# Expert rows beyond 256 in pieces of 128, and the values of two contexts computed in the router's gap

## The chip, the cores and the metric

The kernel runs on one core of one Trainium2 chip. The metric is the device time of one execution in microseconds; the figure before the change is the median of three runs. A profile is one such execution taken apart by the hardware profiler, with its own span. The engines are named as in the profile: PE is TensorE's matmul, PEld its weight load, DVE is VectorE, ACT ScalarE, POOL GpSimd, and SP SyncE, which here only issues DMAs.

## What is computed

Two decoder layers over x (B = 4 sequences of S = 512 rows, D = 256 columns, fp32), each with a layer normalization after every residual addition. The second attention of both layers looks at a context of S2 = 1601 rows per sequence. The feed-forward part of the first layer is a mixture of eight experts, of which each row uses two. Cut to what the change touches:

```python
# layer 0, mixture of experts, 2048 rows
probs = softmax(x @ Wr + br)                      # 8 experts
topw, topi = top_k(probs, 2); topw /= sum(topw)
def expert(x, e):                                 # FF = 1024
    h = gelu(x @ Wi[e] + bi[e]) * sigmoid(x @ Wg[e] + bg[e])
    r = x + (h @ Wo[e] + bo[e])
    return normalized(r) * gamma[e] + beta[e]
x = layernorm(x + sum over the two picks of topw * expert(x, pick))
# layer 1, self attention (16 heads of 16), then cross attention
Q = rope(x @ Wq.T + bq); K = rope(ctx @ Wk.T + bk); V = ctx @ Wv.T + bv
x = layernorm(x + softmax(mask(Q K^T / 4)) V @ Wo.T + bo)
# then a feed-forward part with dequantized weights
```

## The kernel before, in words

The stages follow one another in time: the first attention of layer 0 (0 to about 153 us of the span), its cross attention with the router of each sequence (to 487), a gap in which the last router result is turned into lists of rows (to 523), the experts (to 1023), the self and cross attention of layer 1 (to 2286), and the last feed-forward part (to 2438). Expert, cross-attention and self-attention stages are written under a manual schedule: each engine runs its instructions in the order in which the program issues them.

**Router and lists.** `route(b)` (L457) computes the logits of sequence b on PE, picks two experts per row on DVE, and multiplies the picks with a triangular matrix (L507) to rank each row within its expert. `scatter(b)` (L528) then writes the rows of x to a list `xs` in DRAM, one region of 2048 rows per expert, with eight indirect DMAs that POOL issues (L534). For the last sequence nothing else fills PE meanwhile. `blocks_left` (L539) counts what each expert has beyond its first 256 rows, and makes the tables `wrow` (which expert's weights) and `xrow` (which rows) of the dynamic blocks, and `yrows`, with which layer 1 fetches its results.

**Blocks.** Every expert has one block of 256 rows whose place is known (8 "first" blocks), and 15 dynamic blocks of 256 rows go where the counts say: 23 in all, however the rows fall. A block needs three weight tiles of its expert: eWi and eWg (1028 KB each, biases behind the matrix) and eWo (1408 KB, with bo, gamma and beta behind it). For a first block SP loads them from a fixed place; for a dynamic block POOL issues indirect DMAs (L397). The functions per block are:

- `begin(i)` (L830): the loads of the rows, xb, and of eWi and eWg. The rows are issued first.
- `turned` (L849): four transposes of xb on PE (L854), copied to xbT by DVE.
- `first_half` (L861): issues the load of eWo; then eWi and eWg times xbT, 256 columns wide, Gelu and Sigmoid on ACT (L883), their product on DVE (L886), and the addition of bo to xb on POOL (L889).
- `second_half` (L892): g times eWo into one bank, the residual addition on DVE (L899), the normalization, gamma and beta on POOL (L910, L911), and the store to `ys` by SP (L912).

The loop (L1002 to L1016) interleaves them: loads of block i+1, first half of block i, transposes of block i+1, second half of block i-1. The buffers are two for each weight, three for xb. So a block's weights arrive while the block before is computed, and `attention_first`, a generator of small preparations for layer 1, is advanced once per block.

**Values of the contexts.** Layer 1's cross attention runs in units (b, g): sequence b, a group g of four heads. Side work is cut into items that are spread over the units in lists named `extras` and `quiet`; loads stand in `starts`. `context(b, keys, values)` (L1173) makes the items of context b: `key` projects, rotates and stores a chunk of keys; `value` (L1186) projects 128 rows of the context with the weight xaV and copies them to `vals[b % 2]` (ACT, L1191). Contexts 0 and 1 are done early; in `later` (L1613) the keys of contexts 2 and 3 and their values, 13 tiles each, are spread over the cross units of b = 0, 1 and 2. A tile takes two matmul calls, four PE passes as the profile counts them, of 256 columns.

Of the kernel before, what the change touches and what calls it, by code (L numbers as in the profile page):

```python
# [9 lines left out]
F32 = mybir.dt.float32  # L10
# [29 lines left out]
def decoder(ctx: ExitStack, tc: tile.TileContext, a: dict, out: bass.AP):  # L40
# [345 lines left out]
    NDYN = 2 * B * S // BLK - 1  # L386
    ys = tc.dram_tile(((E + NDYN) * BLK, D), F32, name="ys")

# [28 lines left out]
    for name, n in (("iota", E), ("base", E), ("more", E - 1), ("upto", E * E), ("dyn", NDYN), ("p", 2)):  # L417
        fields[name] = cmoe[:, at_ : at_ + n]
        at_ += n
# [119 lines left out]
    def blocks_left():  # L539
# [5 lines left out]
        more = prt.tile([P, E, E - 1], F32, tag="more", name="more")  # L545
        nc.vector.tensor_tensor(
            more,
            n[:, :, None].to_broadcast([P, E, E - 1]),
            fields["more"][:, None, :].to_broadcast([P, E, E - 1]),
# [4 lines left out]
        upto = prt.tile([P, E, E], F32, tag="upto", name="upto")  # L554
# [8 lines left out]
        past = prt.tile([P, NDYN, E], F32, tag="past", name="past")  # L563
# [12 lines left out]
        nc.vector.tensor_scalar(j, j, 1.0, float(E - 1), ALU.add, ALU.min)  # L576
# [4 lines left out]
        nc.vector.tensor_scalar(xf, j, float(BLK), None, ALU.mult)  # L581
# [5 lines left out]
        xrow = prt.tile([P, 2, NDYN], I32, tag="xrow", name="xrow")  # L587
        for h in range(2):
            nc.vector.tensor_scalar(xrow[:, h, :], xf, fields["p"][:, h : h + 1], None, ALU.add)
# [6 lines left out]
        nc.vector.tensor_tensor(yf, yf, eks, ALU.subtract)  # L596
# [8 lines left out]
        return wrow, xrow  # L605


    with tc.tile_pool(name="p2", bufs=2) as p2, ExitStack() as ordered:
# [135 lines left out]

        def tail():
            if tails and next(tails[0], tails) is tails:
                tails.pop(0)
# [21 lines left out]
        while tails:  # L769
            tail()  # L770
        ordered.close()
        scatter(B - 1, lambda inst: unordered("xs", inst))
        wrow, xrow = blocks_left()
# [8 lines left out]
    VW = HD + 1  # L782
# [38 lines left out]
    with tc.tile_pool(name="p3", bufs=2) as p3, ExitStack() as ordered:  # L821
# [8 lines left out]
        def begin(i):  # L830

            e = i if i < E else wrow[:, i - E : i - E + 1]
            xb = p3.tile([P, 2, D], F32, tag="xb", name="xb", bufs=3)
            if i < E:
                nc.sync.dma_start(
                    xb, xs[i * B * S : i * B * S + BLK, :].rearrange("(h p) d -> p h d", p=P)
                )
            else:
                for h in range(2):
                    nc.gpsimd.indirect_dma_start(  # L840
                        xb[:, h, :],
                        None,
                        xs,
                        bass.IndirectOffsetOnAxis(ap=xrow[:, h, i - E : i - E + 1], axis=0),
                    )
            wi, wg = expert_first[i] if i < 2 else load_expert(e, expert_in, pmw)
            return i, e, wi, wg, xb

        def turned(i, e, wi, wg, xb):  # L849
            ps = bank()  # L850
            pv = ps.rearrange("p (c n) -> p c n", c=2)
            for c in range(2):
                for h in range(2):
                    nc.tensor.transpose(  # L854
                        pv[:, c, h * P : (h + 1) * P], xb[:, h, c * P : (c + 1) * P], ident
                    )
            xbT = p3.tile([P, 2, BLK], F32, tag="xbT", name="xbT")
            nc.vector.tensor_copy(xbT, pv)  # L858
            return i, e, wi, wg, xb, xbT

        def first_half(i, e, wi, wg, xb, xbT):  # L861

            (wo,) = load_expert(e, ("eWo",), p3)
            g = p3.tile([P, NF, BLK], F32, tag="g", name="g")
            for w, func in ((wi, AF.Gelu), (wg, AF.Sigmoid)):
                for f0 in range(0, NF, 4):
                    ps = wide()
                    pv = ps.rearrange("p a (h n) -> p (a h) n", n=BLK)
                    dst = g[:, f0 : f0 + 4, :]
                    if w is wg:  # L870
                        dst = p3.tile([P, 4, BLK], F32, tag="sg", name="sg")
                    for k in range(4):
                        f = f0 + k
# [3 lines left out]
                                (w[:, c * FF + f * P : c * FF + (f + 1) * P], xbT[:, c, :])  # L877
# [3 lines left out]
                    for k in range(4):  # L881
                        bias = w[:, 2 * FF + f0 + k : 2 * FF + f0 + k + 1]
                        nc.scalar.activation(dst[:, k, :], pv[:, k, :], func, bias=bias)  # L883
                    if w is wg:
                        part = g[:, f0 : f0 + 4, :]
                        nc.vector.tensor_tensor(part, part, dst, ALU.mult)  # L886

            bo = wo[:, None, NF * D : NF * D + D].to_broadcast([P, 2, D])
            nc.gpsimd.tensor_tensor(xb, xb, bo, ALU.add)  # L889
            return i, wo, xb, g  # L890

        def second_half(i, wo, xb, g):  # L892
            ps = bank()
            pv = ps.rearrange("p (h d) -> p h d", d=D)
            for h in range(2):
                blk = slice(h * P, (h + 1) * P)
                mm(pv[:, h, :], [(g[:, f, blk], wo[:, f * D : (f + 1) * D]) for f in range(NF)])
            r = p3.tile([P, 2, D], F32, tag="rb", name="rb")
            nc.vector.tensor_tensor(r, pv, xb, ALU.add)  # L899
            mv = moments(r, 2)  # L900
            rs = rstd_of(mv, eps12, 2)
            for h in range(2):
                nc.vector.tensor_scalar(
                    r[:, h, :], r[:, h, :], mv[:, h, 0:1], rs[:, h : h + 1], ALU.subtract, ALU.mult
                )
            gam, bet = (
                wo[:, None, (NF + k) * D : (NF + k + 1) * D].to_broadcast([P, 2, D]) for k in (1, 2)
            )
            eng = nc.vector if i == E + NDYN - 1 else nc.gpsimd
            eng.tensor_tensor(r, r, gam, ALU.mult)  # L910
            eng.tensor_tensor(r, r, bet, ALU.add)  # L911
            nc.sync.dma_start(ys[i * BLK : (i + 1) * BLK, :].rearrange("(h p) d -> p h d", p=P), r)  # L912
# [87 lines left out]
        ready = {}  # L1000
        ordered.enter_context(tc.manual_schedule())
        n = E + NDYN  # L1002
        read = [begin(0), begin(1)]
        more = attention_first()
        begun = first_half(*turned(*read.pop(0)))
        nxt = turned(*read.pop(0))
        for i in range(1, n):
            if i + 1 < n:
                read.append(begin(i + 1))
            half = first_half(*nxt)  # L1010
            if i + 1 < n:
                nxt = turned(*read.pop(0))
            second_half(*begun)
            begun = half
            next(more, None)
        second_half(*begun)  # L1016
# [9 lines left out]
    with ExitStack() as s4:  # L1026
# [146 lines left out]
        def context(b, keys, values, here=None):  # L1173
# [20 lines left out]
            for i in sorted({*keys, *values}):  # L1194
# [5 lines left out]
                eng = nc.gpsimd if here is None else nc.vector  # L1200
# [403 lines left out]
        for f in keys0[0:2] + values1 + add + keys0[4:6] + turn:  # L1604
            f()
# [5 lines left out]
        for i, (n0, n1) in enumerate(((0, 4), (4, 6), (6, 7), (7, 8))):  # L1611
            extras[i] = ([k1_, q1_, rows1] if i == 0 else []) + keys1[n0:n1] + extras[i]
        later = [  # L1613
            context(2, range(4), ()) + context(3, range(2), ()),
            context(3, range(2, 4), ()) + context(2, (), range(4)),
            context(3, (), range(4)),
        ]
# [124 lines left out]
def _constants():  # L1742
# [11 lines left out]
    ndyn = 2 * B * S // (2 * P) - 1  # L1754
# [3 lines left out]
        np.arange(1, E) * 2 * P,  # L1758
# [95 lines left out]
```

## Time and profile before

| | |
|---|---|
| median of three runs | 2437.68 us (2436.15 to 2438.79) |
| the profiled execution, whole | 2439.88 us |
| its span | 2438.0 us |
| its mean granted clock | 0.97 |
| PE busy | 2344.4 us (96%) |
| DMA | 215.84 MB, mean 89 GB/s |

The second part of the page shows the span in 40 slices, about 61 us each, busy tenths per slice:

```profile
PE   7898999959999999989999999999999999999998
PEclk9999999969999999989999997999999999999999
DMA  8300311145667555351211210112110110100100
GB/s 307 150 1 3 124 54 45 49 143 186 247 239 266 198 204 201 124 164 50 66 48 35 95 36 5 39 51 60 51 37 16 45 36 16 30 34 18 31 9 26
```

PE is full almost everywhere; the slice with a 5, the ninth, holds the router's gap, and there the granted clock is lower too. The experts are the slices nine to seventeen, where the DMA engines work most.

A line of a timeline below gives the start, the length, the engine, the line of the kernel and the operation, the output tile and the inputs, the shape, and in brackets how long the engine had been idle before it and who released it. A pass of the expert matmuls is short, so the length of a group of them, from one group's start to the next one's, is the better measure: the ends are modelled, and a printed length overlaps the next group a little.

### The profile page before, as it was taken

To read this page: it belongs to the slowest core of one execution; us is meant where nothing else is said; L and a number is where in the kernel's file an instruction comes from. 1 tells how busy PE (TensorE), PEld (TensorE's weight loads), DVE (VectorE), ACT (ScalarE), POOL (GpSimd) and SP (SyncE) were. 2 spreads that over 40 slices of the span, in tenths; PEclk is the share of its full clock that TensorE was granted. 3 is DMA by queue.
4 is the path that set the end of the run, shared out by engine and by line. 5 is a ranking of instruction groups with operands and counts; after the bars stand their busy time and mean duration, and the time that the engine had idled before them with its cause. 6 is when DMAs were issued, how large, how long until landed. Compare 5 with 4: busy or idle time off the path is not lost.

```text
span 2438.0 us, 34867 instructions
## 1 busy us (share of the span) xinstructions
PE 2344.4 (96%) x13928; PEld 1328.2 (54%) x13928; DVE 1211.7 (50%) x2854; ACT 1073.5 (44%) x1996; POOL 422.7 (17%) x429
## 2 busy tenths in 40 slices
PE   7898999959999999989999999999999999999998
PEld 4767677748888888843333334333333333333256
DVE  1333334322222233266656667666666666677334
ACT  1111122114444544424555453655666566566730
POOL 1010001121144433345130010222110010000000
PEclk9999999969999999989999997999999999999999
DMA  8300311145667555351211210112110110100100
GB/s 307 150 1 3 124 54 45 49 143 186 247 239 266 198 204 201 124 164 50 66 48 35 95 36 5 39 51 60 51 37 16 45 36 16 30 34 18 31 9 26
DMA packets 76112, 215.84 MB, mean 89 GB/s; under 512 B 11816, under 2 KB 35630, under 8 KB 66862
## 3 DMA queue, kind: packets, MB, share of 16 engines
q1 hardware_dynamic: 61790, 133.04, 16.1%
q0 software_dynamic: 10992, 65.54, 7.3%
q10 hardware_dynamic: 3168, 15.03, 1.8%
q8 instruction: 110, 1.80, 0.3%
q14 instruction: 52, 0.43, 0.1%
HBM read 171.53 MB, written 53.21 MB: 92 GB/s over the span
## 4 chain that ended last, share of the span: by engine, by line
PE 51%; ACT 1%; DVE 1%; issue 0%; DVEq 0%; ACTq 0%
PE s L1310 23%; PE one L202 12%; PE po L1337 11%; PE s L202 2%; PE s L1320 1%; PE one L1295 1%; PE one L1358 1%; ACT x L171 0%; ACT ex L1324 0%; DVE one L1269 0%; PE one L1379 0%; PE one L1477 0%; PE one L1400 0%; DVE pm L1267 0%; DVE st L156 0%
## 5 line engine op out<-in xcount | busy, mean ns | idle before, releaser
L1324 ACT ACTIVATE ex<-s 128x512 f32<-128x512 f32 (+1 forms) x1062 | 577.9, 594 | 466.9 <-PE s L1310 236.7
L1267 DVE TENSOR_REDUCE pm<-one 128x1 f32<-128x512 f32 x768 | 493.7, 685 | 174.5 <-PE s L1310 123.3
L1310 PE MATMUL s<-q,kc 32*128 32x512 f32 x1612 | 524.1, 640 | 0.2 <-ACT ex L1324 0.2
L202 PE MATMUL one<-kc,qt 32*128 32x512 f32 (+1 forms) x2048 | 483.8, 564 | 0.3 <-DVE pm L1267 0.3
L1310 PEld LDWEIGHTS s<-q,kc 32*128 32x128 f32 x1612 | 161.6, 179 | 210.9 <-issue 175.5
L1337 PE MATMUL po<-ex,v 128*32 128x256 f32 (+3 forms) x2472 | 245.1, 465 | 0.3 <-ACT ot L1350 0.3
L1269 DVE CUSTOM_DVE_ANT_0 one<-one,c_diagq 128x512 f32<-128x512 f32 x256 | 171.9, 716 | 75.6 <-PE one L202 63.5
L1310 PE MATMUL s<-q,ks 32*128 32x512 f32 x512 | 179.8, 650 | 5.3 <-ACT ex L1324 4.9
L1337 PEld LDWEIGHTS po<-ex,v 128*32 128x32 f32 (+1 forms) x2472 | 49.8, 108 | 232.2 <-issue 225.5
L886 DVE TENSOR_TENSOR g<-g,sg 128x1024 f32<-128x1024 f32 x46 | 57.2, 1243 | 235.8 <-ACT sg L883 235.7
L202 PE MATMUL wide<-xbT,eWi 128*128 128x256 f32 x736 | 168.9, 389 | 4.0 <-DVE xbT L858 4.0
L202 PEld LDWEIGHTS one<-kc,qt 32*128 32x128 f32 x2048 | 164.2, 188 | 11.6 <-DVE pm L1267 7.9
L202 PE MATMUL wide<-xbT,eWg 128*128 128x256 f32 x736 | 162.6, 379 | 0.0
L202 PE MATMUL bank<-eWo,g 128*128 128x256 f32 x736 | 162.5, 379 | 0.0
L202 PEld LDWEIGHTS wide<-xbT,eWi 128*128 128x128 f32 x736 | 143.5, 196 | 25.8 <-issue 4.2
L202 PE MATMUL one<-ks,qt 32*128 32x512 f32 x512 | 152.6, 665 | 3.7 <-ACT raw L1182 2.7
L202 PEld LDWEIGHTS wide<-xbT,eWg 128*128 128x128 f32 x736 | 139.7, 190 | 19.2 <-ACT g L883 0.2
L1150 POOL TENSOR_TENSOR raw<-raw,c_cos 128x512 f32<-128x512 f32 (+1 forms) x32 | 34.9, 1092 | 660.5 <-DVE swp L1149 578.1
L202 PEld LDWEIGHTS bank<-eWo,g 128*128 128x128 f32 x736 | 138.2, 190 | 17.9
L883 ACT ACTIVATE g<-wide,eWi 128x256 f32<-128x256 f32 x184 | 71.7, 476 | 72.3 <-PE wide L202 69.7
L1310 PEld LDWEIGHTS s<-q,ks 32*128 32x128 f32 x512 | 53.8, 185 | 83.4 <-issue 62.0
L202 PE MATMUL wide<-ctxT,q 128*128 128x512 f32 (+1 forms) x256 | 91.3, 510 | 0.8 <-DVE q L649 0.8
(319 smaller groups left out, 2988.4 us busy)
## 6 DMA issues: line engine op xcount, KB each, us to landing
xs<-zero SPq DMA_DIRECT2D x32, 512.0 KB
kc<-kcd SPq DMA_DIRECT2D x16, 800.5 KB
eWo<-in_eWo SPq DMA_DIRECT2D x8, 1408.0 KB
cx<-in_ctxT SPq DMA_DIRECT2D x18, 512.0 KB
eWi<-in_eWi SPq DMA_DIRECT2D x8, 1028.0 KB
eWg<-in_eWg SPq DMA_DIRECT2D x8, 1028.0 KB
qt<-qd SPq DMA_DIRECT2D x32, 256.0 KB
ctxT<-in_ctxT SPq DMA_DIRECT2D x4, 1601.0 KB
```

The costliest lines, as they stand in the source:

```text
L202: nc.tensor.matmul(ps, l, r, start=(i == 0), stop=(i == n - 1))
L883: nc.scalar.activation(dst[:, k, :], pv[:, k, :], func, bias=bias)
L886: nc.vector.tensor_tensor(part, part, dst, ALU.mult)
L1150: eng.tensor_tensor(raw[:, :n], raw[:, :n], cos[:, :n], ALU.mult)
L1267: nc.vector.tensor_reduce(pm[:, t, j, c : c + 1], ps, AX.X, ALU.max)
L1269: nc.vector.tensor_tensor_reduce(out=ps, in0=ps, in1=diagq[:, 384 - t * P : 896 - t * P], scale=1.0, scalar=LOWEST, op0=ALU.add, op1=ALU.m ...
L1295: nc.tensor.transpose(pt[:, t * P : (t + 1) * P], ng.rearrange("p j r -> p (j r)"), ident)
L1310: nc.tensor.matmul(ps[:kn], kt[rows, k * P : k * P + kn], q2[rows, :], start=True, stop=cross)
L1320: nc.tensor.matmul(ps[:, k * P : (k + 1) * P], later_[:, :P], later_[:, P:], start=False, stop=True)
L1324: nc.scalar.activation(ex[:kn, h, :], ps[:kn], AF.Exp)
L1337: nc.tensor.matmul(state["po"][j * 32 : j * 32 + 32, q0:q1], (vals if cross else vself)[b % 2][:kn, k, c0 : c0 + 32], ex[:kn, j % 2, q0:q1 ...
L1358: nc.tensor.transpose(pt[:, t * P : (t + 1) * P], ot[:, t * P : (t + 1) * P], ident)
```

## The change

- **Pieces.** The rows beyond 256 of an expert are cut into pieces of 128, at most 14 per expert; 28 pieces are provided, and a "more" block of the loop holds two of them, each with its own expert's weights. So there are 8 first and 14 more blocks, in an order written out as a string. A more block loads two sets of eWi, eWg and eWo, multiplies each with its 128 columns, and ends each half of 128 rows by itself.
- **Order of the loads.** eWi and eWg of the next block are issued within `first_half`, piece by piece as the buffers are used up. eWo of a block is issued in the `second_half` of the block before, after gamma and beta, and the rows of the block after that, xb, are issued behind it.
- **bo** is added on DVE, in `second_half`.
- **Values.** The 26 value tiles of contexts 2 and 3 are computed between the tails of the last router step: four after its second step, twelve after its sixth, ten after `blocks_left`. They are copied to tiles whose old contents are no longer needed, stored to DRAM (`vd`), and loaded to `vals` when the cross units of the sequence before them begin. The items of `later` are keys alone.
- **Tables.** `blocks_left` stands before the last scatter, inside the manual schedule, and its tables are larger; `count` is made and not used.
- **Start of layer 1.** Half of context 0's key chunks are rotated on POOL, and the first items are in another order.

```diff
-    NDYN = 2 * B * S // BLK - 1
-    ys = tc.dram_tile(((E + NDYN) * BLK, D), F32, name="ys")
+    NMORE = (B * S - BLK) // P
+    NDYN = 2 * NMORE
+    ys = tc.dram_tile((E * BLK + NDYN * P, D), F32, name="ys")
...
+        xaV = weight(p2, "xaV")
+        values, places = [], {}
+        def rows_of_values():
+            big = p2in.tile([P, NT * S2], F32, tag="fs", name="v23")
+            rest = p2in.tile([P, KHALF * D], F32, tag="ctxa", name="v2")
...
+            for b_ in (2, 3):
+                nc.vector.memset(places[b_, NKT - 1], 0.0)
+            for t in (big[:, : 22 * VROW], rest[:, : 4 * VROW]):
+                t = t.rearrange("p (k r) -> p k r", r=VROW)
+                nc.vector.memset(t[:, :, NH * VW :], 0.0)
...
+                nc.vector.memset(heads[:, :, :, HD : HD + 1], 1.0)
+        def value(b, k):
+            kn = kn_of(k)
+            ps = bank()[:, :D]
+            mm(ps[:kn], [(ctxTs[b][:, c, k * P : k * P + kn], xaV[:, c, :]) for c in range(2)])
+            dst = places[b, k][:kn, : NH * VW].rearrange("p (h r) -> p h r", r=VW)
+            nc.scalar.copy(dst[:, :, :HD], ps[:kn].rearrange("p (h r) -> p h r", r=HD))
+            if b == 2 and k == NKT - 1:
+                nc.sync.dma_start(vd[2][:, : 9 * VROW], big_of(2, 0, 9))
+                nc.sync.dma_start(vd[2][:, 9 * VROW :], big_of(2, 9, NKT))
+            if b == 3 and k == NKT - 1:
+                nc.sync.dma_start(vd[3], big_of(3, 0, NKT))
...
-        while tails:
-            tail()
+        values = [lambda b=b, k=k: value(b, k) for b in (2, 3) for k in range(NKT)]
+        for n in (0, 4, 0, 0, 0, 12, 0, 0, 0, 0, 0):
+            if n == 4:
+                tail()
+                rows_of_values()
+            else:
+                tail()
+            for f in values[:n]:
+                f()
+            values = values[n:]
+        wrow, xrow, count = blocks_left()
+        for f in values:
+            f()
         ordered.close()
         scatter(B - 1, lambda inst: unordered("xs", inst))
-        wrow, xrow = blocks_left()
...
+        def first_half(block, nxt):
+            xbT = loaded.pop((block, "xT"))
+            g = p3.tile([P, NF, BLK], F32, tag="g", name="g")
+            for name, func in (("eWi", AF.Gelu), ("eWg", AF.Sigmoid)):
+                ws = loaded.pop((block, name))
+                for i in range(2):
+                    if len(ws) == 1:
+                        w, fs_, cols = ws[0], range(4 * i, 4 * i + 4), slice(0, BLK)
+                    else:
+                        w, fs_, cols = ws[i], range(NF), slice(i * P, (i + 1) * P)
...
+                    if nxt and (nxt, name) not in first_loads:
+                        weights_of(nxt, name, i)
+        def second_half(block, nxt, after):
...
+            for h in range(2):
+                wo = wos[h % len(wos)]
+                blk = slice(h * P, (h + 1) * P)
+                mm(pv[:, h, :], [(g[:, f, blk], wo[:, f * D : (f + 1) * D]) for f in range(NF)])
+                if len(wos) == 1 and h == 0:
+                    continue
...
+                eng = nc.gpsimd if nxt else nc.vector
+                eng.tensor_tensor(r[:, hs], r[:, hs], gam, ALU.mult)
+                eng.tensor_tensor(r[:, hs], r[:, hs], bet, ALU.add)
...
+                for half in range(2) if len(wos) == 1 else (h,):
+                    if nxt:
+                        weights_of(nxt, "eWo", half)
+            if after:
+                rows_of(after)
...
+            for i, b in enumerate(blocks):
+                first_half(b, get(i + 1))
+                if get(i + 1):
+                    turned(get(i + 1))
+                if i:
+                    second_half(blocks[i - 1], b, get(i + 2))
+                elif get(2):
+                    rows_of(get(2))
+                next(work, None)
+            second_half(blocks[-1], None, None)
+        order = "ffmfmfmmfmfmmfmfmm" + "m" * 4
...
-                eng = nc.gpsimd if here is None else nc.vector
+                eng = nc.gpsimd if here is None or i % 2 else nc.vector
...
-        for f in keys0[0:2] + values1 + add + keys0[4:6] + turn:
+        for f in keys0[0:2] + values1[:8] + add + values1[8:] + turn + keys0[4:6]:
...
-        later = [
-            context(2, range(4), ()) + context(3, range(2), ()),
-            context(3, range(2, 4), ()) + context(2, (), range(4)),
-            context(3, (), range(4)),
-        ]
+        later = [context(2, range(4), ()), context(3, range(4), ())]
+        for b in (2, 3):
+            starts[index[b - 1, 1, True]].append(
+                lambda b=b: nc.sync.dma_start(vals[b % 2].rearrange("p k r -> p (k r)"), vd[b])
+            )
```

## The prediction

> **What bounds the kernel now.** I read the busy table first, then the span cut into windows at the stage borders (columns: length, then busy us and instruction count of PE, PEld, DVE, ACT, POOL, then granted clock, DMA share, GB/s).
>
> ```profile
> PE 2344.4 (96%) x13928; PEld 1328.2 (54%) x13928; DVE 1211.7 (50%) x2854; ACT 1073.5 (44%) x1996; POOL 422.7 (17%) x429
> 487.00:523.00 36.00, 10.12 (x40) 8.65 (x39) 13.73 (x76) 3.03 (x5) 13.43 (x14) 0.54 0.40 130
> 523.00:1023.00 500.00, 496.04 (x2308) 433.24 (x2308) 135.91 (x263) 236.07 (x457) 159.82 (x158) 0.99 0.57 208
> 1445.00:2286.00 841.00, 840.53 (x6476) 302.53 (x6468) 578.96 (x1063) 488.70 (x919) 90.20 (x74) 0.98 0.11 34
> ```
>
> TensorE is the bound in both stages that matter: the blocks of the expert list (523 to 1023) and the cross units (1445 to 2286). Work taken from PE there shortens the span by its own length, and a wait put on PE there lengthens it. Between them lies the router's gap: 36 us, 10 of them busy, at about half the clock.
>
> One block, in the timeline of PE:
>
> ```profile
> 788.10 7.07 PE L202 MATMUL wide<-xbT,eWg 128*128 128x256 f32 x32
> 795.01 0.60 PE L854 MATMUL bank<-ident,xb 128*128 128x128 f32 x4
> 795.44 7.07 PE L202 MATMUL bank<-eWo,g 128*128 128x256 f32 x32
> 802.35 7.07 PE L202 MATMUL wide<-xbT,eWi 128*128 128x256 f32 x32
> ```
>
> The starts give 6.91 us for 32 passes (0.216 each), 0.43 us for four transposes, and so 21.16 us a block.
>
> **Blocks: what is taken away.** Of 23 blocks 22 stay: 8 first, 14 more. A more block has two pieces with weights of their own, so eWi and eWg take 128 passes of 128 columns instead of 64 of 256. Rows of that width, from the first attention:
>
> ```profile
> 204.03 1.05 PE L202 MATMUL bank<-mid,back 128*128 128x128 f32 x8
> 204.93 0.60 PE L202 MATMUL bank<-rs,inv 128*128 128x256 f32 x2
> ```
>
> 0.90 / 8 = 0.1125 us a pass. A more block is 128 x 0.1115 (mean with the neighbouring eight, 0.111) + 32 x 0.216 + 0.43 = 21.6 us. All blocks: 8 x 21.16 + 14 x 21.6 = 471.7 against 23 x 21.16 = 486.7, **-15 us**. Were a pass to cost the group's mean, 26.2 / 192 = 0.136 us, which holds half-clock stretches too, the term is +29; I take the full-clock rows, since the block stage stands at 0.99.
>
> [...]
>
> **Blocks: what is added, the loads.** Two weight sets are 2 x 3464 KB a more block, by POOL's queue, against 3464 before. Order matters more than bytes. Before, the row gather of a block was issued ahead of its three weights. Now POOL runs, after the second half of block i-1: gamma, beta, both eWo pieces of block i, and only then the rows of block i+2, whose transposes PE reaches one first half later. The old block's chain after its second half (PE done at 781.19):
>
> ```profile
> 781.45 0.69 DVE L899 TENSOR_TENSOR rb<-bank,xb 128x512 f32<-128x512 f32 x1 [3.92 <-issue]
> 785.87 1.27 POOL L911 TENSOR_TENSOR rb<-rb,eWo 128x512 f32<-128x512 f32 x1
> 787.29 1.00 POOL L840 DMA_INDIRECT xb<-xs,xrow  x1
> ```
>
> If block i-1 is a first block, beta ends 6.0 us after PE; the bo addition moved from POOL to DVE adds one 0.69; eWo is issued at +6.8. What a load then takes:
>
> ```profile
> 705.22 0.95 POOL L397 DMA_INDIRECT eWi<-in_eWi,wrow  x1 [0.30 <-issue]
> 707.73 0.95 POOL L397 DMA_INDIRECT eWo<-in_eWo,wrow  x1 [0.30 <-issue]
> 718.36 1.27 POOL L889 TENSOR_TENSOR xb<-xb,eWo 128x512 f32<-128x512 f32 x1 [9.67 <-DMA eWo<-in_eWo,wrow]
> 709.00:717.00 8.00, 8.00 (x41) 7.05 (x40) 3.05 (x3) 3.86 (x8) 0.00 (x0) 1.00 0.90 362
> ```
>
> Three weights (3.55 MB) land 13.1 us after the first issue, while the queue moves 362 GB/s; 3.55 MB at that rate are 9.8, so starting and landing take some 2 us (the rest is issue pitch). Two eWo and the rows are 2.88 + 0.26 MB, 8.7 us at 362: rows at +17.3, at best +16.5 (the packets show up to 400 GB/s in mid-load). PE wants them after one first half: +13.8 to +14.3. A stall of 2.4 to 3.4 us, and the clock pays again:
>
> ```profile
> 545.46 10.01 PE L202 MATMUL wide<-xbT,eWi 128*128 128x256 f32 x32 [3.17 <-DVE xbT L858]
> 555.31 7.07 PE L202 MATMUL wide<-xbT,eWg 128*128 128x256 f32 x32
> 1048.69 6.24 PE L202 MATMUL one<-xaV,cx 128*128 128x256 f32 x20 [2.07 <-DMA cx<-in_ctxT]
> ```
>
> After 3.17 us idle, 32 passes take 2.9 us more than warm ones; after 2.07 idle, 20 take 1.9 more (6.24 against 20 x 0.216). So some 5 us each. It happens where block i-1 is first and block i more: at the transposes of blocks 4, 6, 8, 11, 13, 16, 18 (counted from 0). 8 and 13 are first blocks whose rows come by SP beside the two eWo, so I take half for them: 5 x 5.2 + 2 x 2.6 = **+31**. Bounds: 0, if the rows slip in beside the weights, and 7 x 6.3 = 44.
>
> [...]
>
> After a more block the chain starts half a second half earlier, on 256-column tiles: no stall by the same sum. There the next limit is bytes: 7.1 MB of weights and 0.5 of rows at 362 GB/s are 21 us against 21.6 of PE, so loads just hide; the cover is under 1 us. I put +2 for the border cases (0 to 8).
>
> **The end of the list.** The last block's eWo pieces need the buffers and POOL turn of block 20, so nothing hides them: issue about 1 us after PE, start and landing 2, 1.44 MB at 362 GB/s 4.0: 7 us idle, 1.9 of clock: **+8** (4 to 10).
>
> **Gelu and sigmoid**: 32 activations of 128 columns instead of 16 of 256, at an estimated 0.31 against 0.39 us: 10 us a block on ACT, beside 21.6 of PE, free. POOL loses the bo addition and gains three issues at 1.26; its last gather lands as above.
>
> **Values.** 26 value tiles of contexts 2 and 3 leave the cross units: 104 passes. There
>
> ```profile
> L202 PE MATMUL one<-xaV,cx 128*128 128x256 f32 x64 | 18.1, 405 | 0.0
> ```
>
> 18.1 / 64 = 0.283, x 104 = **-29.4**, whole, because PE idles 0.5 us of those 841. What takes their place there: two reloads of 1.9 MB in a stage that moves 34 GB/s, hidden.
>
> In the gap they are not free:
>
> ```profile
> 489.90 1.38 DVE L726 TENSOR_SCALAR x<-r,mv,rstd 128x256 f32<-128x256 f32 x4 [0.60 <-ACT rstd L127]
> 505.49 0.64 PE L202 MATMUL bank<-both,before 128*128 128x32 f32 x2 [5.75 <-DVE both L492]
> ```
>
> The first four stand before the transposes; the third waits for ACT's copy, which waits for memsets behind that normalization on DVE. So the transposes start some 4 to 5 us after 490.37. Then twelve stand between router and rank matmul, in 5.75 us of idle: 48 passes are 10.4 us warm, some 13 with the 2.9 of a cold start above. 4 + 13 - 5.75 = **+11** (6 to 15) for the rank matmul, hence for rows, scatters and the first block. The last ten run behind it under the eight scatters (about 10 us of POOL); their stores precede the first rows on SP.
>
> **Start of the last attention**: the order of the first items changes and half the rotation of context 0 goes to POOL, which is 30 of 49 us busy there: -1 (-5 to +4).
>
> **Sum.** -15 + 31 + 2 + 8 - 29.4 + 11 - 1 = +7 (rounded) on the profiled span of 2438.0, whose run took 2439.9, 2.2 above the median of 2437.68. On the median: **2445**.
>
> **Rivals.** *Rows come in time*: the DMA engines share between small rows and eWo, or the stall stays under a microsecond and the clock holds. For it: no row shows whether a small gather must wait for the large load issued ahead of it, and the stall is only 3 us. Against: before, the weight issued last of three also landed last, after 13.1 us. Then the +31 goes: 2414; with half of it, 2429. *The more blocks become bound by their loads*: slower. For it: the cover is under 1 us, and the whole 13.1 us row gives only 270 GB/s, at which 7.6 MB take 28. It decides once the mean rate falls under 7.6 / 21.6 = 352 GB/s; at 320 a block takes 23.8, x 14 = +31, of which part is the stalls already counted: 2465. Against: 362 with 0.90 of the share. *The gap swallows the values* (slower too): memsets, half clock and vd stores ahead of the first rows cost 20 instead of 11, 2454. *Narrow passes at 0.136*: +44, 2489. That the work is not removed I exclude: block count and items are fixed.
>
> **Chances.** Stalls as worked 0.45 (own range 2436 to 2456), rows in time or half of it 0.30, load-bound 0.15, gap 0.06, narrow passes 0.04. Three executions spread 2.6 us, so about 0.2% (4.9 us) is what can be told from no change. Under 2432.8: the rows-in-time case nearly whole and a little of the others, 0.32; between, 0.11 from the low part of the first; above 2442.6: 0.57. The range leaves out the lowest third of the first rival and the dearest of the slow ones: 2416 to 2470.
>
> **What would show it.** In the changed profile: PE idle of 2 to 3.5 us before the transposes of blocks 4, 6, 11, 16, 18, released by the DMA of xb, with a first half-clock group behind each; about 7 us before the last eWo passes; more blocks at 21.6 us elsewhere; the rank matmul near 516; no passes of xaV in the cross units, which end 29 us sooner against their start. A block stage under 475 us would refute the stalls; one over 520, with waits on eWi or eWg in the last eight blocks, would be the loads.

## The result, and the profile after

The changed kernel takes 2505.55 us (median of four runs, 2500.83 to 2509.26) against 2438.23 before (four runs, 2436.15 to 2443.3): a ratio of 1.0282, 95% interval 1.0266 to 1.0298. It is slower by 67 us, where 7 were forecast. The profiled execution has a span of 2502.2 us against 2438.0, and the difference of 64.2 is what is accounted for below.

The page of the changed kernel, busy table and slices (62.5 us each):

```profile
PE 2357.1 (94%) x14940; PEld 1360.4 (54%) x14940; DVE 1219.4 (49%) x2891; ACT 1101.7 (44%) x2214; POOL 471.6 (19%) x491
...
PE   7998999888988999987999999999999999999998
```

PE's row has eights now in the expert stage (slices nine to eighteen), where all slices behind the gap were nines before, and a seven after it, in slice nineteen, where layer 1 starts. The windows, cut at four marks: the last product before the gap, the first transposes of the expert stage, the last expert product, the first finished attention unit. First the kernel before, from the second mark on, then the changed one:

```profile
523.00:1024.00 501.00, 496.11 (x2309) 433.27 (x2309) 136.72 (x265) 236.07 (x457) 159.82 (x158) 0.99 0.57 208
1024.00:1130.20 106.20, 99.22 (x394) 50.23 (x394) 65.05 (x179) 38.01 (x81) 47.53 (x46) 0.87 0.41 124
1130.20:2438.00 1307.80, 1289.53 (x9106) 504.27 (x9102) 824.63 (x1878) 708.16 (x1330) 161.37 (x145) 0.98 0.12 38
```

```profile
487.50:534.80 47.30, 34.84 (x144) 28.75 (x143) 17.18 (x82) 12.61 (x31) 15.25 (x16) 0.82 0.26 98
534.80:1094.90 560.10, 503.38 (x3104) 454.57 (x3104) 156.51 (x322) 263.10 (x675) 185.65 (x195) 0.95 0.73 275
1094.90:1211.40 116.50, 97.19 (x394) 49.52 (x394) 50.00 (x153) 37.63 (x81) 68.62 (x70) 0.87 0.38 111
1211.40:2502.20 1290.80, 1272.16 (x9218) 495.55 (x9214) 824.06 (x1878) 700.19 (x1305) 161.43 (x145) 0.98 0.12 39
```

So: the gap +11.8, the experts +59, the start of layer 1 +10, the rest -17. The forecast had +11, +26, -1 and -29. In the expert stage PE is busy 503 us in 560; before it was 496 in 501.

What the stage lost can be read at block 6, in the timeline of PE and of POOL:

```profile
660.60 7.07 PE L202 MATMUL wide<-xbT,eWg 128*128 128x256 f32 x32
672.12 1.16 PE L926 MATMUL bank<-ident,xb 128*128 128x128 f32 x4 [4.44 <-DMA xb<-xs,xrow]
673.07 6.10 PE L202 MATMUL bank<-eWo,g 128*128 128x256 f32 x16
679.74 3.72 PE L202 MATMUL bank<-eWo,g 128*128 128x256 f32 x16 [0.57 <-DVE rb L984]
```

```profile
659.10 1.27 POOL L998 TENSOR_TENSOR rb<-rb,eWo 128x512 f32<-128x512 f32 x1
660.51 0.97 POOL L400 DMA_INDIRECT eWo<-in_eWo,wrow  x1
661.79 0.95 POOL L400 DMA_INDIRECT eWo<-in_eWo,wrow  x1 [0.30 <-issue]
663.05 0.96 POOL L915 DMA_INDIRECT xb<-xs,xrow  x1 [0.30 <-issue]
```

The rows are issued third and land last: PE waits 4.44 us for them, the 16 passes behind run at about half the clock (6.10 us against 3.72 for the next 16), and between the two halves of the second product stands a wait of 0.57 on DVE that no block had before. Over the stage I added up PE's idle times: those longer than 1.2 us are 45.5 us (before 3.2), the shorter ones 10.7 (0.8), and PE's busy time inside half-clock stretches, halved, is 21.6 (6.4). With the -15 of the passes that makes +52 of the +59. The rest is an estimate: 16 passes in front of a wait end 0.16 us later than half an unbroken group of 32 (3.62 against 3.46), the 16 behind one take 0.10 more (3.56, at full clock), and the stage has 27 waits where it had 2, so some 6 us.

The narrow passes themselves, in a more block without a wait before them (from one start to the next 7.15 us for 64):

```profile
839.15 7.31 PE L202 MATMUL wide<-xbT,eWg 128*128 128x128 f32 x64
846.30 0.60 PE L926 MATMUL bank<-ident,xb 128*128 128x128 f32 x4
```

### The profile page after: what moved, and what is told of

Same layout as the page of the kernel before. It is cut to its first block, busy times and chain, and to the rows that moved or that the text cites. A ratio compares the mean times of both kernels' runs of the same rounds, so it can differ in the third digit from the quotient of the medians.

```text
span 2502.2 us, 37420 instructions
## 1 busy us (share of the span) xinstructions
PE 2357.1 (94%) x14940; PEld 1360.4 (54%) x14940; DVE 1219.4 (49%) x2891; ACT 1101.7 (44%) x2214; POOL 471.6 (19%) x491
## 3 DMA queue, kind: packets, MB, share of 16 engines
q0 software_dynamic: 16512, 111.39, 11.8%
## 4 chain that ended last, share of the span: by engine, by line
PE 49%; DVE 1%; ACT 1%; issue 0%; DVEq 0%; ACTq 0%
PE s L1421 22%; PE po L1448 11%; PE one L202 10%; PE s L202 2%; PE s L1431 1%; PE one L1406 1%; PE one L1469 1%; ACT x L171 0%; ACT ex L1435 0%; DVE pm L1378 0%; DVE one L1380 0%; PE one L1490 0%; PE one L1588 0%; PE one L1511 0%; DVE nb L166 0%
## 5 line engine op out<-in xcount | busy, mean ns | idle before, releaser
L1448 PE MATMUL po<-ex,v 128*32 128x256 f32 (+3 forms) x2688 | 251.5, 443 | 0.3 <-ACT ot L1461 0.3
L1380 DVE CUSTOM_DVE_ANT_0 one<-one,c_diagq 128x512 f32<-128x512 f32 x256 | 171.8, 716 | 75.4 <-PE one L202 62.5
L202 PE MATMUL bank<-eWo,g 128*128 128x256 f32 x704 | 175.6, 409 | 20.5 <-DMA eWo<-in_eWo,wrow 11.7
L202 PEld LDWEIGHTS one<-kc,qt 32*128 32x128 f32 x2048 | 164.4, 188 | 11.9 <-DVE pm L1378 7.8
L202 PE MATMUL wide<-xbT,eWi 128*128 128x128 f32 (+1 forms) x1152 | 161.8, 301 | 4.0 <-DVE xbT L930 4.0
L202 PEld LDWEIGHTS wide<-xbT,eWi 128*128 128x128 f32 x1152 | 152.2, 193 | 13.1 <-issue 4.1
L202 PE MATMUL wide<-xbT,eWg 128*128 128x128 f32 (+1 forms) x1152 | 158.9, 298 | 0.0
L202 PEld LDWEIGHTS wide<-xbT,eWg 128*128 128x128 f32 x1152 | 149.8, 192 | 6.6
L1261 POOL TENSOR_TENSOR raw<-raw,c_cos 128x512 f32<-128x512 f32 (+1 forms) x32 | 34.9, 1092 | 628.0 <-DVE swp L1260 568.5
L98 ACT ACTIVATE sd<-mv,eps 128x1 f32<-128x1 f32 (+2 forms) x40 | 11.8, 295 | 217.0 <-DVE mv L109 217.0
L962 ACT ACTIVATE g<-wide,eWi 128x128 f32<-128x128 f32 (+1 forms) x288 | 85.5, 407 | 47.4 <-PE wide L202 39.1
```

The lines of the kernel that those rows point to most:

```text
L202: nc.tensor.matmul(ps, l, r, start=(i == 0), stop=(i == n - 1))
L1261: eng.tensor_tensor(raw[:, :n], raw[:, :n], cos[:, :n], ALU.mult)
L1380: nc.vector.tensor_tensor_reduce(out=ps, in0=ps, in1=diagq[:, 384 - t * P : 896 - t * P], scale=1.0, scalar=LOWEST, op0=ALU.add, op1=ALU.m ...
L1448: nc.tensor.matmul(state["po"][j * 32 : j * 32 + 32, q0:q1], (vals if cross else vself)[b % 2][:kn, k, c0 : c0 + 32], ex[:kn, j % 2, q0:q1 ...
```

## The experiments

Each is the changed kernel with the edit shown, or builds on an earlier one where it says so. The block stage of four kernels with the same block code took 559.5, 552.0, 550.2 and 561.9 us from the first transposes to the last eWo pass (the changed kernel and the runs on the rotation, the values and the split below), so differences under some 12 us there are not read from the length alone.

### The rotation back on DVE

```diff
-                eng = nc.gpsimd if here is None or i % 2 else nc.vector
+                eng = nc.gpsimd if here is None else nc.vector
```

> Half of context 0's key chunks go back from POOL to DVE; nothing else. Theory: the rotations on POOL stand behind the sums of sequence 1, hold the four raw tiles, and so cause the 12.86 us of idle PE at 1133 with the half clock behind it; then this idle goes and the way from the last expert pass to the first finished attention unit falls from 117.1 to 107 us or less: span 2502.2 to some 2490. Rival: the idle comes from the new order of the first items or from the DMAs of that stretch; then it stays, and the span is 2500 or more.

In the changed kernel, the timeline of all engines around the start of layer 1:

```profile
1136.50 0.72 POOL L1211 TENSOR_TENSOR x<-x,y 128x256 f32<-128x256 f32 x1
1137.18 1.26 POOL L1261 TENSOR_TENSOR raw<-raw,xT 128x512 f32<-128x512 f32 x1
...
1145.30 0.60 ACT L1235 ACTIVATE raw<-one 128x512 f32<-128x512 f32 x1 [16.65 <-DMA kcd<-raw]
...
1145.95 2.07 PE L202 MATMUL one<-qkvV,xT 128*128 128x256 f32 x4 [12.86 <-ACT raw L1235]
```

The chunks of context 0 were projected by 1129, but POOL begins to rotate them at 1137.18, behind its sums for sequence 1 (L1211). Until they are stored the raw tiles stay taken, ACT waits 16.65 us for one, and PE 12.86. With the edit that idle is gone:

```profile
1086.70:1191.70 105.00, 96.75 (x394) 49.24 (x394) 63.94 (x177) 38.37 (x81) 46.86 (x46) 0.89 0.41 123
```

105 us instead of 116.5 for the stretch, and from the last expert pass to the end 1392.7 instead of 1407.8 (11.5 of these 15 us in the stretch itself). The span is 2478.8; 7.5 of its 23.4 us lie in the block stage, whose code is unchanged here, and are not the edit's. The theory held.

### The order of the blocks

```diff
-        order = "ffmfmfmmfmfmmfmfmm" + "m" * 4
+        order = "ff" + "m" * 14 + "f" * 6
```

> Order of the blocks alone: ff, then all 14 more blocks, then 6 first. Theory: the long waits for rows stand only where a first block is followed by a more block, so of seven one is left (the transposes of block 4), and the last block, now a first one, finds its eWo loaded; PE idle over 1.2 us in the block stage falls from some 42 us to under 15, and the stage from 560 to about 515 to 525 us. Rival: the loads are the bound (7.6 MB a more block); then a run of 14 more blocks waits for eWi, eWg or eWo throughout, a more block takes 24 us or longer with DMA waits, and the stage stays at 550 or more.

Span 2488.7, block stage 535.6. The one wait that was to stay stands where it should (4.10 us before the transposes of block 4), and the six others are gone; four smaller ones of 1.8 to 2.9 us came in the run of more blocks. So a first block followed by a more block is what makes the long wait. The stage is 10 us over the upper end of the theory, 14 under the rival's: of the blocks in the run most take 22.5 to 24.6 us and two 27, their waits being for rows and not for weights. But the end of the list went the wrong way:

```profile
1037.53 7.07 PE L202 MATMUL bank<-eWo,g 128*128 128x256 f32 x32
1057.78 9.44 PE L202 MATMUL bank<-eWo,g 128*128 128x256 f32 x32 [13.19 <-DMA eWo<-in_eWo]
```

I had put the wait at the end down to the buffers. Here two first blocks use one eWo tile each, so the buffer is free, and SP loads it; it is issued at 1051.60 only, behind the store of ys (1051.12), which waits for beta. So the order in the program is enough to make this wait, as for the rows. In the changed kernel both reasons hold at once: the last block's first eWo piece is issued at 1077.99, right behind beta (1077.00), which is also the last to read the old contents of its buffer.

### The rows ahead of eWo

```diff
                 nc.vector.tensor_tensor(r[:, hs], pv[:, hs], xb[:, hs], ALU.add)
+                if after and h == 1:
+                    rows_of(after)
...
                         weights_of(nxt, "eWo", half)
-            if after:
-                rows_of(after)
```

> The gather of the rows is issued as soon as the residual addition has freed its buffer, ahead of gamma, beta and the two eWo; nothing else. Theory: order in the queue is the cause, so the waits on xb (blocks 4, 6, 8, 9, 11, 16, 18: 4.0 to 5.8 us each) go with their half clock, some 40 us off the stage of 560; what is left is the wait at the end of the list, and perhaps 1 to 2 us on eWo. Rival: bytes are the cause, the wait moves from xb to eWo of the same blocks in nearly the same length, and the stage falls by less than 15 us.

Block stage 514.3 instead of 559.5, span 2457.2. Block 6 again:

```profile
646.39 7.07 PE L202 MATMUL wide<-xbT,eWg 128*128 128x256 f32 x32
653.29 0.60 PE L926 MATMUL bank<-ident,xb 128*128 128x128 f32 x4
653.73 3.62 PE L202 MATMUL bank<-eWo,g 128*128 128x256 f32 x16
657.93 3.72 PE L202 MATMUL bank<-eWo,g 128*128 128x256 f32 x16 [0.58 <-DVE rb L984]
```

No wait for the rows, and no passes at half clock. All waits on xb over 1 us are gone; on eWo 0.7 to 1.7 us are left in some eight places, and 7.2 at the end of the list. Not the bytes but their order was at fault: the same bytes move in a stage 45 us shorter.

### Two banks, and then two tiles

```diff
-            ps = bank()
-            pv = ps.rearrange("p (h d) -> p h d", d=D)
+            pv = wide()[:, :, :D]
```

> The two halves of a block's second product go to two banks of PSUM instead of one; nothing else. Theory: the second half waits for DVE's addition that reads the first half's part of the same bank, 0.57 to 1.18 us in each of 14 more blocks; these idles go, and a more block in the undisturbed end of the list falls from some 24 to 23 us, the stage by about 9. Rival: the wait is for the weights or for g and stays; no change. Against both: the tile takes one of three double banks, so the first products could wait for ACT, a loss of a few microseconds.

No effect: the block stage takes 554.5, and the wait on DVE between the halves is still 0.57 to 0.61 us. The next run gives the second half a tile of its own:

```diff
             for h in range(2):
+                if h and len(wos) == 2:
+                    ps = bank()
+                    pv = ps.rearrange("p (h d) -> p h d", d=D)
                 wo = wos[h % len(wos)]
```

> The second half of a more block's second product gets a PSUM tile of its own, instead of the other part of one tile (in the run before, two banks of one tile left the 0.57 us wait on DVE as it was). Theory: the wait is the program's dependence on the tile, so with two tiles it goes: 14 waits of 0.57 to 1.18 us, some 9 us of the stage of 560. Rival: the wait is on the chip's side (weights, g) and stays, under 3 us.

The same passes in the undisturbed end of the list, first with two banks of one tile, then with two tiles:

```profile
1019.83 3.72 PE L202 MATMUL wide<-eWo,g 128*128 128x256 f32 x16 [0.61 <-DVE rb L983]
```

```profile
1013.31 3.72 PE L202 MATMUL bank<-eWo,g 128*128 128x256 f32 x16 [0.28 <-DVE xbT L930]
```

PE's idle times under 1.2 us fall from 10.7 to 2.4 us over the stage, and the stage takes 546.7. It was the program's dependence on the tile: one part of it is read while the other is to be written.

### The values back in the cross units

The 26 items go back to `later` as before, and none is computed in the gap.

> The changed kernel with the 26 value tiles of contexts 2 and 3 back in the cross units: the blocks alone. Theory (values moved at little gain): the first transposes of the block stage fall back from 534.8 to about 523, and the stretch from the first finished attention unit to the end grows back from 1291 to about 1308; net +5, span some 2507. Rival (the predicted price, 29.4 us saved against 11 paid): span some 2520.

The first transposes come at 521.8 (534.8 with the move), and from the first finished unit to the end it takes 1306.3 us (1290.8): +15.5 for the values in the units, -13.0 in the gap. By these two numbers the move was worth some 3 us (the first transposes of other kernels with the same gap came at 529.1 to 534.2, so up to 8). The span, 2496.0, is even lower than with the move, since the block stage happened to take 550.2.

The 15.5 holds a difference that is not the move's. From the first finished unit to the sixteenth runs the self attention of layer 1, whose code is the same in both: it took 354.8 us here and 358.0 in the changed kernel, and PE's busy time at half clock, halved, was 11.9 and 15.4 us in it. In the cross units themselves the move gave 1.6 us in the first one (56.9 to 55.3) and 16.3 in the next twelve (644.3 to 628.0): some 18. So the cost in the gap was priced about rightly and the gain was not: 18 for 29.4. Where the difference went shows in the groups of PE over these twelve units, from the end of the first on, before (1546 to 2190) and after (1625 to 2253):

```profile
L1310 PE MATMUL s<-q,kc 32*128 32x512 f32 x1160 | 368.7, 640 | 0.2 <-ACT ex L1324 0.2
...
L1337 PE MATMUL po<-ex,v 128*32 128x256 f32 x1200 | 95.9, 391 | 0.0
L1337 PE MATMUL po<-ex,v 128*32 128x512 f32 x552 | 73.5, 605 | 0.0
```

```profile
L1421 PE MATMUL s<-q,kc 32*128 32x512 f32 x1158 | 374.7, 641 | 0.8 <-ACT ex L1435 0.8
...
L1448 PE MATMUL po<-ex,v 128*32 128x256 f32 x1600 | 127.8, 391 | 0.0
L1448 PE MATMUL po<-ex,v 128*32 128x512 f32 x352 | 46.9, 605 | 0.0
```

At a step without a side item the kernel splits the product with the values in two halves of 256 columns, so that PE has something between the scores. 200 wide passes became 400 narrow ones, and the two groups together grew from 169.4 to 174.7 us: +5.3. The scores stretched by 6.0 with as many passes. That is 11 of the 14 us missing there (29.4 for 15.7, before against after).

### The products with the values never split

```diff
-                    elif not filled:
+                    elif not filled and not u[2]:
```

> In the cross units, the product with the values is never split in two halves of 256 columns, also at steps that have no side item. Theory: a step without an item costs more by its split alone (8 passes of 0.133 us against 16 of 0.080, +0.21 us a step, about 25 steps more than before): all the steps without an item gain it, some 100 steps, and the cross units fall by 10 to 25 us. Rival: the split fills PE while ACT's exponents are awaited; then taking it away costs time in the cross units, 5 us or more, and the price of a step without an item lies in that wait and not in the split.

The rival held, more strongly than it was put: span 2531.9. Four units, the second to the fifth, in the changed kernel and with the edit:

```profile
1624.70:1835.50 210.80, 210.80 (x1692) 73.35 (x1688) 146.25 (x271) 126.06 (x232) 35.32 (x32) 1.00 0.13 40
```

```profile
1623.30:1842.50 219.20, 219.20 (x1452) 74.68 (x1448) 144.33 (x271) 125.75 (x232) 35.25 (x32) 1.00 0.13 39
```

8.4 us more in fewer passes, with PE shown busy throughout. A step without an item leaves a hole in PE's work; the split covers part of it, and an item covers it too. The lengths of the steps show it, counted in the same units from the first pass of one step's product with the values to that of the next: the median of the 24 steps with a value tile alone is 4.20 us (before), of the 94 bare steps 3.91 without the split (this run) and 3.49 with it (the changed kernel). The four passes of a tile are 0.86 us of PE at 0.216 each, yet they lengthen a step by 0.29 if it is not split, and by 0.71 over a split one. 26 times 0.71 is 18.5, close to the 18 of the run before. So PE's busy time there is not all work, and passes that are taken out give back only a part of their length.

### The three edits together

Rotation, rows and two tiles.

> Three edits together: context 0's rotation back on DVE, the rows ahead of eWo, and a tile of its own for each half of the second product. If they act on separate waits they add: -15 (rotation, by its run from the last expert pass on), -45 (rows, in the block stage), and -9 (tiles) on 2502.2 give a span of 2433. If the rows' gain and the tiles' gain eat each other (a faster block makes its loads late), 2440 or more, with waits on eWo or eWi in the more blocks.

Span 2443.0, in the upper of the two cases: the block stage takes 512.5, hardly less than with the rows alone (514.3), though the short idles are down to 4.1 us. What the tiles gave came back as eWo that is later: waits of 1.3 to 2.2 us at five blocks, and 7.87 at the end.

### eWo earlier behind a first block

On the three edits:

```diff
+            if nxt and len(wos) == 1:
+                weights_of(nxt, "eWo", 0)
             ps = bank()
...
-                for half in range(2) if len(wos) == 1 else (h,):
+                for half in (h,):
...
-        order = "ffmfmfmmfmfmmfmfmm" + "m" * 4
+        order = "ffmfmfmmfmmmf" + "m" * 7 + "ff"
```

> On the kernel with the three edits: after a first block, the next block's first eWo piece is issued ahead of that block's normalization (its buffer has long been free), and two first blocks stand at the end of the list. Theory: what is left of the stage's excess is eWo that comes late, 6 to 8 us at the end of the list and 1.3 to 2.2 us behind five first blocks; both go, and from the first transposes to the last eWo pass it falls from 512.5 to 500 or less. Rival: the loads of seven more blocks in a row are the bound once nothing else is; then the waits return there and the stage stays at 508 or more.

Block stage 490.0, span 2424.5; but for the 3.17 us of the first product, one wait over 1.2 us is left (1.55). The end of the list:

```profile
1002.88 7.07 PE L202 MATMUL wide<-xbT,eWg 128*128 128x256 f32 x32
1009.79 13.98 PE L202 MATMUL bank<-eWo,g 128*128 128x256 f32 x64
```

The last block's eWo passes follow the ones before without a wait. Now the stage is shorter than before the change (500.1), by 10 us of the 15 that narrow passes and one block less should give. Part of this is the clock: in the last two runs below, with the same blocks, it takes 494.7 and 496.9, and half clock costs 5.9 and 8.3 us in it where it costs 3.0 here and 6.4 before the change.

### The values 2, 7 and 17

On the three edits:

```diff
-        for n in (0, 4, 0, 0, 0, 12, 0, 0, 0, 0, 0):
-            if n == 4:
+        for n in (0, 2, 0, 0, 0, 7, 0, 0, 0, 0, 0):
+            if n == 2:
```

> On the kernel with the three edits: the 26 values are placed 2, 7 and 17 instead of 4, 12 and 10. Theory: the rank matmul no longer stands behind values (12 of them took 13.6 us where PE had 5.75 to spare), and the 17 fit under the scatters; the first transposes come at 525 to 528 instead of 534, and the span falls by 6 to 9 from 2443. Rival: the last values now end after the scatters and hold the rows back instead (the first rows wait for the last value); first transposes at 531 or later.

In the changed kernel, and then here, PE from the router to the rank matmul:

```profile
487.53 1.89 PE L202 MATMUL bank<-xaV,ctxT 128*128 128x256 f32 x8
494.10 3.49 PE L202 MATMUL bank<-xaV,ctxT 128*128 128x256 f32 x8 [4.68 <-ACT v L782]
...
504.73 13.62 PE L202 MATMUL bank<-xaV,ctxT 128*128 128x256 f32 x48
518.19 0.30 PE L202 MATMUL bank<-both,before 128*128 128x32 f32 x2
```

```profile
495.97 9.31 PE L202 MATMUL bank<-xaV,ctxT 128*128 128x256 f32 x28
505.11 0.30 PE L202 MATMUL bank<-both,before 128*128 128x32 f32 x2
...
524.29 0.63 PE L926 MATMUL bank<-ident,xb 128*128 128x128 f32 x4 [3.05 <-DMA xb<-xs]
```

The rank matmul is back where it was before (505.49), and the first transposes come at 524.3, 9.7 us sooner than with the three edits alone. Span 2428.1, 14.9 less: 4.4 of it is the block stage (508.1), whose code is the same.

### Both, and the blocks without the values

The last two edits together, on the three:

> Both: if the two act on separate waits, the span is 2443 less 12 to 15 less 6 to 9, some 2420 to 2425, which is faster than the kernel before (2438 by its profile) by 0.5 to 0.7 percent. If one of them only moves a wait, 2430 to 2437 and no difference that the rounds can tell.

Span 2413.5; over repeated runs the ratio to the kernel before is 0.9943, 95% interval 0.9925 to 0.9960 (medians 2420.81 and 2434.34 us). So this version is faster than both kernels, by 0.6% against the one before. The last run takes the values out of it again, with the block edits kept.

> The mended blocks (rotation on DVE, rows ahead of eWo, own tiles, early first eWo piece, two first blocks at the end) with the 26 values back in the cross units. Theory: the values' move is worth some 15 us in the cross units and costs, at 2, 7 and 17 in the gap, about 5 us ahead of the first transposes; without it the first transposes come at 522 to 523 instead of 527.7, the stretch from the first finished attention unit to the end is 1305 to 1308 instead of 1287, and the span is 2421 to 2426, still under 2438. Rival: the move is worth nothing on balance, and the span is within 3 us of the 2413.5 with it.

The ratio is 1.0000, interval 0.9986 to 1.0013. Of the two, first with the values moved and then without, the self attention of layer 1 (first to sixteenth finished unit) and the twelve cross units behind the first:

```profile
1125.70:1480.50 354.80, 345.26 (x2242) 138.54 (x2242) 232.06 (x662) 173.16 (x334) 66.11 (x69) 0.97 0.17 52
1535.80:2163.80 628.00, 627.23 (x5140) 219.07 (x5140) 439.94 (x812) 377.68 (x701) 77.52 (x66) 1.00 0.13 41
```

```profile
1126.20:1487.10 360.90, 351.31 (x2242) 139.17 (x2246) 232.00 (x663) 173.17 (x335) 66.10 (x69) 0.95 0.17 52
1544.00:2187.70 643.70, 643.50 (x5032) 227.29 (x5036) 439.36 (x810) 385.26 (x725) 73.81 (x63) 1.00 0.12 38
```

From the first finished unit to the end it takes 1287.3 us with the move and 1309.2 without, but 6 of these 22 us are the self attention, whose code is the same and whose clock was lower in the second run. The move gives 15.7 us in the twelve units and 1.6 in the one before (55.3 and 56.9), and costs 4.6 ahead of the first transposes (527.7 against 523.1): 12.7, and the medians of the two lie 13.0 apart (2420.81 and 2433.84). The span without it, 2436.1, is 10 over the upper end expected: the saving was underrated by some 3 us, and the rest is the self attention, the blocks and the start of layer 1, whose code did not change. The mended blocks come out even with the old ones (stage 496.9 against 500.1), and the gain of the best version is the values'.

## Why the prediction was wrong, point by point

The profiled span grew by 64.2 us where 7 were forecast. Of the 57 between, some 20 are the stalls on the rows, 9 the waits inside the second halves, 11 the start of layer 1, 12 the values, and 5 the rest.

- **The stalls on the rows: right in mechanism and place, too small.** Of the seven blocks named (4, 6, 8, 11, 13, 16, 18) six waited for their rows, and in place of 13 the eWo passes of block 11 waited (4.08 us). The step that failed is "a stall of 2.4 to 3.4 us": the six measured 4.0 to 5.8, and where SP fetches the rows the wait was no shorter (block 8: 4.01). In block 6 the chain ran as worked, beta at +6.7 and eWo at +6.8 us behind PE, but POOL's four issues spread to +10.6 and the rows landed at +18.3, not +17.3. Two waits more (1.2 and 1.8 us, blocks 3 and 9) came beside them. Stalls and their clock: +33 forecast with the border cases, about +53 measured (35.4 of idle, 17.2 of half clock).
- **Not seen at all: a wait inside the second half.** The two halves of a more block share a PSUM tile, and DVE now reads the first while PE is to write the second. The prediction read the new `second_half` for its loads and not for its tile: 13 waits, 8.8 us, shown by the tile of its own, which took 8.3 us of short waits away.
- **The start of layer 1: "-1 (-5 to +4)", measured +10.** The step counted POOL's busy share, 30 of 49 us, and not what stands in its queue ahead of the rotations. POOL's sums for sequence 1 stood ahead of them.
- **The values: "-29.4, whole, because PE idles 0.5 us".** Measured some 18 in one pair and 17 in the other, counted in the cross units (15.5 and 21.9 with the self attention's clock). PE is shown busy in steps that hold a hole, and the side items were filling it. The profile before could have told the price: its 24 steps with a value tile take 4.20 us and its 70 bare ones 3.49, and 26 x 0.71 is 18.5.
- **The gap: +11 forecast, +11.8 measured,** by the steps named: 4.68 us of wait before the third value, the twelve as 13.6 us, the rank matmul at 518.2 for "near 516", 12.7 late.
- **The end of the list: +8 forecast, about +9 measured** (6.9 and 0.8 of idle and 1.5 of clock); its reason was given as buffers and POOL's turn; the order of issue alone is enough, as the order of the blocks showed.
- **The passes: right.** 64 passes of 128 columns take 7.15 us in the undisturbed blocks, 0.1117 each, for 0.1115.
- **Rivals.** The block stage came out at 560 us, over the 520 that was to be a sign of load-bound blocks, but PE waits for eWi or eWg nowhere in it. Load-bound more blocks are refuted: in the best version four in a row take 22.19 us each without a wait on weights, while the queues move 343 GB/s. Rows in time did not come true by themselves, but by an edit that issues them earlier.

## What to carry to other kernels

When a transfer is moved, work out the order of the whole queue it lands in, issue times and bytes ahead of it, and put the small transfer that is needed next ahead of the large one that is needed later (here the block stage fell from 559.5 to 514.3 us). An engine that shows busy all the time may still hold holes that side work fills (here four passes of 0.86 us lengthened a step by 0.29 us if it is not split, by 0.71 over a split one): price removed work by the difference between steps with it and without it in the same profile, not by its passes. Before a difference between two runs is put down to an edit, look how much of it lies in stages whose code is the same (6 of 22 us in the last pair of runs). When one product is cut in two, look whether both parts share a tile that another engine reads in between (here 13 waits, 8.8 us).

## What the runs showed of the hardware

A wait of PE does not have one price. The first product of the second block waited 3.17 us in both kernels: before, it came with half clock from 544.5 to 551.3 us, 1.0 us ahead of the product's start (545.46) and on; in the changed kernel (556.74) with none, the granted clock being 1.00 from 550 to 620. At the start of layer 1, PE waited 2.07 us for a load before its products with xaV (1048.69, before), with 3.4 us of half clock behind, and 2.08 us for ACT in the changed kernel (1115.37), with none (1.00 from 1115.4 to 1122). In the block stage of the changed kernel, the eight waits of 4.0 to 6.9 us each came with a half-clock stretch of 3.4 or 6.8 us, the four of 1.0 to 1.8 us with none. In the run on the order of the blocks, 16 passes took 5.30 and 5.31 us behind waits of 2.88 and 2.04 us, and 3.62 behind waits of 1.90 and 1.76.

In the attention units it is otherwise. In the changed kernel, stretches of 3.4 us came behind waits of 1.66 and 1.32 us (1303.80 and 1376.45), none behind waits of 1.54 and 1.31 (1487.41 and 1285.11). Near the end of the self attention half clock stood for 20.5 us (1545.1 to 1565.6; before, 27.3 us from 1462.6 on), with PE idle for 0.27 us in the 7 us ahead of it and shown busy throughout it. So a busy row of PE does not mean full speed there. But for the last of each profile, the half-clock stretches of the two kernels last 3.4, 6.8, 10.2, 20.5, 27.3 or 41.0 us. The clock is one reason why the same block code took 550.2 us with the values back in the units (granted clock 0.96) and 559.5 in the changed kernel (0.95), and why the same self attention took 354.8 us in one of the last two runs (0.97) and 360.9 in the other (0.95).
